# Scattering the experts' results to the tokens' places instead of gathering them, with weights fetched further ahead

## The chip, the cores and the metric

The kernel runs on one core of a Trainium2 chip. The core has a matrix engine (PE, with its weight loads shown apart as PEld), a vector engine (DVE), a scalar engine (ACT), GpSimd (POOL) and a queue engine (SP) that here only issues transfers. The engines run side by side and wait for each other through semaphores. The metric is the device time of one run in microseconds (us), the median over runs; lower is better.

## What is computed

Four layers, each a cross attention followed by a mixture of experts, both added to the stream `x` of 4 batches x 512 tokens x 128 channels. The context has 154 tokens per batch.

```python
x = x + L0_xattn(layernorm(x), ctx)                # one similarity, weights sim -> features -> W_qv
x = x + L0_ffn(layernorm(x))                       # 8 experts, the best 2 of each token, silu gate, hidden 512
x = x + L1_xattn(ctx, ctx, layernorm(x), mask)     # 16 heads of 8
x = x + L1_ffn(layernorm(x))                       # best 1 of 8, with a capacity, gelu, hidden 512
x = x + L2_xattn(layernorm(x), ctx)                # 16 heads of 64, gated
x = x + L2_ffn(layernorm(x))                       # best 2 of 8, gelu, hidden 256
x = x + L3_xattn(layernorm(x), ctx, ctx)           # 16 heads of 64
x = x + L3_ffn(layernorm(x))                       # best 2 of 8, relu, hidden 512

# an expert layer, in short
top_w, top_i = top_k(x @ Wg + bg, k);  w = softmax(top_w)
y[t] = sum over k of  w[t,k] * (act(x[t] @ W1[e] + b1[e]) @ W2[e] + b2[e])   with e = top_i[t,k]
```

## The kernel before

All arithmetic is in float32. A token tile is 128 tokens; there are 16 of them (`NT`), 4 per batch (`NI`). The stream `x` stays in SBUF.

**Experts by blocks.** Every expert layer is done in two halves, batches 0 and 1, then 2 and 3 (`NH` = 8 tiles each). `route` (L651) works out, for one half, which expert each token goes to and at which row of a DRAM buffer it is to lie, so that the rows of one expert fill whole blocks of 128. A half has a fixed number of blocks, `BLK`: 23 with two experts a token, 15 with one, which is enough for any routing; unused rows hold what was there before. `route` is a generator, advanced a step at a time beside other work. It ends with a list of `scatter` calls (L721): one GpSimd indirect transfer moves 128 normalized token rows to their rows of `buf`, 512 bytes each.

`experts` (L825) then walks over the blocks. `load` (L835) brings four blocks of token rows, after all scatters of the half; `tokens` transposes them; `up` (L855) reads the block's expert from a register on SP and PE, loads this expert's up weights into one of three `w` buffers and multiplies; `down` (L882) applies the activation, multiplies by the down weights and copies the result to `ys`, which SP stores as a block to `ybuf` (L928). `up` of a step is emitted ahead of `down` of the step before. A step is one block in layer 0 and two in the others (`PER`).

**Back to the tokens.** `gather` (L948) reads `ybuf` back by rows: for each of a half's tiles and each of its one or two experts, one GpSimd indirect transfer of 128 rows (L953), each after all stores of the half. `combine` (L965) adds the rows times the gate's weight to `x`.

**Order.** The main loop (L1356) emits: attention; the first half's experts, with the second half's routing beside them; the first half's gathers; the next layer's keys and values (`at.early`); the second half's experts, and between their steps the first half's combination, statistics (`stats`, whose last operation runs on POOL), normalization and queries (`at.late`); then the next layer's attention, beside whose first tiles the second half is gathered and combined. Indirect transfers are not started at once: they wait in `rows_due`, and `row_transfers` (L641) takes some off, each tied to a piece of other work. In attention (`narrow_period`, `wide_period`) PE, ACT and partly DVE run in the order written; elsewhere a scheduler orders what is emitted. Each engine, and each transfer queue, works in order. SP carries all plain transfers: weights, token blocks, result blocks, and in attention the reciprocal sums that go through DRAM (`rd`, `rep`, L346 and L348). POOL carries the indirect ones and `rstd` (L236).

## Time and profile before

| what | us |
|---|---|
| runs, median of 3 | 1359.35 (1351.47 to 1362.25) |
| the profiled execution | 1282.47 |
| its span, first to last instruction | 1280.8 |
| layer 0 attention | 0 to 106 |
| layer 0 experts, first and second half | 106 to 195, 195 to 262 |
| layer 1 attention, experts | 262 to 478, 478 to 575 |
| layer 2 attention, experts | 575 to 803, 803 to 911 |
| layer 3 attention, experts | 911 to 1125, 1125 to 1252 |
| after the last expert block | 1252 to 1281 |

The stage bounds are read off the timeline and are not sharp, since the stages overlap. The profile is one execution; the mean TensorE clock granted in it was 0.917 of full speed. The costliest indirect transfers in it are 112 scatters (L722, 109.6 us of POOL) and 112 gathers (L953, 106.7 us); SP issues 110 result stores (L928), 44 token loads (L840) and 168 loads of up weights (L869). A line of the profile reads: engine, line, operation, output and inputs, count; a bracket gives the idle time of the engine just before and what ended it.

### The profile page before, as it was taken

How to read it: one execution, taken by the hardware profiler on the slowest of the kernel's cores; microseconds unless marked ns; L12 is line 12 of the kernel's file. 1: busy time of each engine (PE TensorE's matmuls, PEld its weight loads, DVE VectorE, ACT ScalarE, POOL GpSimd, SP SyncE). 2: the span in 40 equal slices, each digit the busy share in tenths (PEclk: the TensorE clock that was granted, in tenths of full speed). 3: DMA queues.
4: the chain of work that ended last, by engine and by line, in shares of the span. 5: the costliest groups of instructions: out<-in, count | busy, mean ns of one | idle time of the engine just before them, and what ended most of it. 6: DMA issues, size and time to landing. Idle time of an engine off the chain costs nothing.

```text
span 1280.8 us, 26318 instructions
## 1 busy us (share of the span) xinstructions
PE 1089.4 (85%) x9351; PEld 896.9 (70%) x9351; DVE 731.6 (57%) x2012; ACT 565.3 (44%) x2264; POOL 253.6 (20%) x281
## 2 busy tenths in 40 slices
PE   4787998977878888889999998966899999899990
PEld 3657998933435448787878777855778788789890
DVE  6554646567666763335665776424476576646352
ACT  2113433454554543546656565321656665532230
POOL 2041315023000010232000004045220000402334
PEclk8767999988898988998999999887999999999996
DMA  7023786721100314433112214444421111334762
GB/s 228 1 81 113 216 253 189 207 94 25 23 19 26 100 38 119 133 110 84 35 35 55 64 37 123 123 150 133 127 55 45 41 35 35 109 95 143 209 191 60
DMA packets 136064, 126.77 MB, mean 99 GB/s; under 512 B 12538, under 2 KB 115583, under 8 KB 135551
## 3 DMA queue, kind: packets, MB, share of 16 engines
q1 hardware_dynamic: 128767, 110.39, 30.5%
q0 software_dynamic: 7168, 14.69, 3.9%
q8 instruction: 77, 1.26, 0.4%
q14 instruction: 52, 0.43, 0.1%
HBM read 101.31 MB, written 23.72 MB: 98 GB/s over the span
## 4 chain that ended last, share of the span: by engine, by line
PE 59%; DVE 12%; DMA 9%; issue 8%; ACT 5%; POOL 5%; SPq 2%; POOLq 0%; DVEq 0%
PE sc L877 11%; PE av L916 6%; PE tr L371 6%; PE sc L607 5%; PE av L408 5%; PE tr L425 5%; PE sc L592 3%; DMA yg<-ybuf,su 3%; POOL yg L953 3%; ACT probs L308 3%; DVE nm L294 3%; PE sc L1175 2%; DMA w<-in_up 2%; PE av L390 2%; PE tr L358 2%
## 5 line engine op out<-in xcount | busy, mean ns | idle before, releaser
L308 ACT ACTIVATE probs<-sc,nm 128x154 f32<-128x154 f32 x768 | 286.9, 403 | 162.7 <-DVE nm L294 162.5
L877 PE MATMUL sc<-tokT,w 128*128 128x128 f32 x1528 | 201.3, 286 | 8.7 <-DMA w<-in_up 3.6
L877 PEld LDWEIGHTS sc<-tokT,w 128*128 128x128 f32 x1528 | 189.0, 200 | 15.5 <-ACT eg L900 5.2
L294 DVE TENSOR_REDUCE nm<-sc 128x6 f32<-128x924 f32 x144 | 142.6, 1007 | 74.8 <-PE sc L607 49.1
L308 ACT ACTIVATION_READ_ACCUMULATOR probs<-sc,nm 128x1 f32 x768 | 168.3, 219 | 0.0
L916 PE MATMUL av<-w,hT 128*128 x1160 | 155.3, 279 | 3.2 <-DVE hT L905 2.5
L953 POOL DMA_INDIRECT yg<-ybuf,su x112 | 106.7, 952 | 246.5 <-ACT pT L267 59.9
L722 POOL DMA_INDIRECT buf<-xn,su x112 | 109.6, 979 | 227.0 <-DVE eb L745 97.3
L916 PEld LDWEIGHTS av<-w,hT 128*128 128x128 f32 x1160 | 141.9, 193 | 8.9 <-issue 4.7
L236 POOL TENSOR_TENSOR rstd<-ve,nhalf 128x4 f32<-128x4 f32 x32 | 33.0, 1032 | 547.3 <-DVE ve L234 429.6
L264 DVE COPY pT<-tr 128x512 f32<-128x512 f32 x160 | 106.9, 684 | 45.3 <-PE tr L371 41.5
L408 PE MATMUL av<-pT,vm 128*64 128x128 f32 (+1 forms) x1536 | 106.2, 284 | 22.5 <-DVE pT L264 22.4
L371 PE MATMUL tr<-ident,probs 128*128 128x128 f32 x768 | 123.1, 291 | 1.5 <-DVE rT L337 1.5
L371 PEld LDWEIGHTS tr<-ident,probs 128*128 128x128 f32 x768 | 86.1, 146 | 33.4 <-issue 21.7
L408 PEld LDWEIGHTS av<-pT,vm 128*64 128x64 f32 (+1 forms) x1536 | 63.8, 126 | 55.7 <-DVE pT L264 30.9
L900 ACT ACTIVATE eg<-sc,w 128x128 f32<-128x128 f32 x184 | 52.9, 368 | 89.5 <-PE sc L877 82.1
L607 PE MATMUL sc<-kT,qT 64*128 64x154 f32 x1024 | 87.1, 308 | 4.8 <-ACT probs L308 4.8
L905 DVE SCALAR_TENSOR_TENSOR hT<-sc,w,eg 128x128 f32<-128x128 f32 x184 | 56.2, 342 | 51.0 <-ACT eg L900 51.0
L607 PEld LDWEIGHTS sc<-kT,qT 64*128 64x128 f32 x1024 | 71.3, 189 | 15.8 <-issue 9.9
L592 PE MATMUL sc<-xnT,wq 128*128 128x128 f32 x512 | 73.6, 303 | 4.7 <-ACT probs L308 2.3
L592 PEld LDWEIGHTS sc<-xnT,wq 128*128 128x128 f32 x512 | 67.3, 212 | 10.2 <-issue 3.6
L425 PE MATMUL tr<-wo,aT 128*128 128x128 f32 x512 | 66.2, 284 | 1.6 <-DVE xnT L256 1.3
(255 smaller groups left out, 1432.2 us busy)
## 6 DMA issues: line engine op xcount, KB each, us to landing
w<-in_up SPq DMA_DIRECT2D x46, 516.0 KB
w<-in_up SPq DMA_DIRECT2D x76, 258.0 KB
rep<-rd SPq DMA_DIRECT2D x64, 256.0 KB
tok<-buf SPq DMA_DIRECT2D x36, 256.0 KB
ybuf<-ys SPq DMA_DIRECT2D x58, 128.0 KB
w<-in_down SPq DMA_DIRECT2D x3, 2048.0 KB
w<-in_up SPq DMA_DIRECT2D x46, 128.0 KB
ybuf<-ys SPq DMA_DIRECT2D x52, 64.0 KB
```

Of the source, the lines that this page charges most:

```text
L264: return nc.vector.tensor_copy(o, i)
L294: nc.vector.tensor_reduce(self.at.heads(self.nm, g, n), self.sc[g][:, :, 0 : n * S2].rearrange("p j (s k) -> p j s k", s=n), AX.X, ALU.max ...
L308: nc.scalar.activation(self.pr[:, h, :], self.sc[g][:, j, s * S2 : (s + 1) * S2], AF.Exp, bias=self.nm[:, h : h + 1], accum_out=self.rs[:, ...
L371: nc.tensor.transpose(q[:, t * P : (t + 1) * P], self.pr[:, h, 0:P], ident)
L408: nc.tensor.matmul(av[rows, cols], v, self.pT[n][:, t, :], start=False, stop=last)
L425: nc.tensor.matmul(o[:, 0:D], self.aT[:, c, :], self.at.wo[:, c, :], start=(c == 0), stop=(c == self.nb - 1))
L592: nc.tensor.matmul(sc[:, c // 4, c % 4 * P : (c % 4 + 1) * P], wq[:, c * P : (c + 1) * P], at.xnT[:, i * P : (i + 1) * P], start=True, sto ...
L607: nc.tensor.matmul(sc[:, j, s * S2 : (s + 1) * S2], at.qT[i][rows, c, :], at.kT[rows, c, :], start=True, stop=True)
L722: ins = nc.gpsimd.indirect_dma_start(out=buf[half], out_offset=bass.IndirectOffsetOnAxis(ap=su[:, t : t + 1], axis=0), in_=xns[t // NI][:, ...
L877: nc.tensor.matmul(dst, w[:, b, at : at + P], xT, start=True, stop=True)
L916: nc.tensor.matmul(y[:, b * D : (b + 1) * D], hT[:, fc, :], w2[:, bass.ds(es[b], 1), fc, :].rearrange("p o d -> p (o d)"), start=(fc == 0) ...
L953: ins = nc.gpsimd.indirect_dma_start(out=yg[:, t, :], out_offset=None, in_=ybuf[half], in_offset=bass.IndirectOffsetOnAxis(ap=su[:, t : t ...
```

## The change

Results take the other way. A token row in `buf` gets two more columns: the token's place in the output and the row of its first expert. When a block is loaded, two DVE operations make of these the row of `ybuf` where each result belongs (`goal`): two rows for a token, one per expert. Rows of no token, or left over from an earlier layer, come out beyond the end. Each block's result then goes to `ybuf` by one indirect transfer on POOL, with a bounds check that skips those rows. The half comes back in plain loads on SP, one a batch, after all results of the half. The gathers and the plain stores are gone.

With it:

- the halves of layer 0 become batch 0, and batches 1 to 3 (15 and 31 blocks); the routing of the second half is taken batch by batch and begun earlier; layer 0's attention gets a written PE order;
- up weights are fetched in groups of one or two steps, alternately into `w` and into a buffer of attention's `probs`, three groups ahead, instead of one step at a time;
- results wait in `results_due`, at most six steps; while scatters are due, these go first, two plus the step's blocks at a time;
- the next layer's first scores are made before the last experts are finished, and the first tokens of a second half wait for the next layer's values on PE;
- several small buffers become single or shared.

```diff
+GROUPS = (((0,), (1, 2, 3)), ((0, 1), (2, 3)), ((0, 1), (2, 3)), ((0, 1), (2, 3)))
+ROW = D + 2
+ROWS = 2 * B * S
+LAG = 6
...
     def route(layer, half, wg, bg, b2):
...
+        for some in ([b] for b in batches) if layer == 0 or half else (batches,):
...
+                rows = rt.tile([P, NI, ROW], F32, tag="xn", name="rows", bufs=4)
+                new.append(norm(x[b], f, rows))
+                nc.vector.tensor_scalar(
+                    rows[:, :, D], place[:, b * NI : (b + 1) * NI], float(-(layer + 1) * ROWS), None, ALU.add
+                )
...
+            if k == 0:
+                for n, rows in enumerate(xns):
+                    nc.vector.tensor_copy(rows[:, :, D + 1], sl[:, n * NI : (n + 1) * NI])
...
-    def experts(layer, half, routed, w2):
+    def experts(layer, half, routed, w2, ahead=()):
...
+        few = UP_WIDTH // (per * width)
+        groups, at = [], 0
+        while at < len(turns):
+            big = len(groups) > 1 and len(groups) % 2 == 0
+            groups.append((turns[at : at + few * (1 + big)], big))
+            at += len(groups[-1][0])
...
+        def fetch(k):
...
+            if big:
+                w = p2.tile([P, H, S2], F32, tag="probs", name="w_more").rearrange("p h k -> p (h k)")
+            else:
+                w = wff.tile([P, UP_WIDTH], F32, tag="w", name="w")
...
+                    nc.sync.dma_start(v[:, b, :], pack[bass.ds(e, 1), :, :].rearrange("o p n -> p (o n)"))
...
+            second = small.tile([P, 4], F32, tag="second", name="second")
+            nc.vector.tensor_tensor(
+                second[:, 0:m], tok[:, 0:m, D + 1], slot[:, 4 * g : 4 * g + m], ALU.not_equal
+            )
+            goal = small.tile([P, 4], U32, tag="goal", name="goal", bufs=6)
+            nc.vector.scalar_tensor_tensor(
+                goal[:, 0:m], tok[:, 0:m, D], float((layer + 1) * ROWS), second[:, 0:m], ALU.add, ALU.add
+            )
...
-            ys = p3.tile([P, 2, D], F32, tag="ys", name="ys")
-            row_transfers(
-                2 * n, nc.vector.tensor_copy(ys[:, 0:n], y[:, 0 : n * D].rearrange("p (b d) -> p b d", b=n))
+            ys = p3.tile([P, 2, D], F32, tag="ys", name="ys", bufs=LAG + 2)
+            done = nc.vector.tensor_copy(ys[:, 0:n], y[:, 0 : n * D].rearrange("p (b d) -> p b d", b=n))
+            results_due.extend(partial(result, j, ys[:, b, :]) for b, j in enumerate(blocks))
+
+            some = min(len(rows_due), 2 + n)
+            row_transfers(some, done)
+            results(2 + n - some)
+            results(len(results_due) - LAG * n)
+
+        def result(j, y):
+
+            ins = nc.gpsimd.indirect_dma_start(
+                out=ybuf[half],
+                out_offset=bass.IndirectOffsetOnAxis(ap=goals[j // 4][:, j % 4 : j % 4 + 1], axis=0),
+                in_=y,
+                in_offset=None,
+                bounds_check=ROWS - 1,
+                oob_is_err=False,
             )
-            rows = ybuf[half][blocks[0] * P : (blocks[0] + n) * P, :]
-            stores.append(nc.sync.dma_start(rows.rearrange("(b p) d -> p b d", p=P), ys[:, 0:n]))
...
-    def gather(half, routed, stores):
...
-    def combine(half, k, i, routed, got):
...
+    def combining(layer, half, routed, stores):
...
+        def get(k):
+            b = batches[k]
+            yg = p2.tile([P, NI, top, D], F32, tag="yg", name="yg")
+            rows = ybuf[half][2 * b * S : 2 * (b + 1) * S, :].rearrange("(i p c) d -> p i c d", p=P, c=2)
+            wait_for(nc.sync.dma_start(yg, rows[:, :, 0:top, :]), stores, "any block may hold these tokens")
+            return yg
+
+        got = {k: get(k) for k in range(min(2, len(batches)))}
...
+        first, second = (Steps(route(layer, half, *gates[layer])) for half in range(2))
+        with tc.manual_schedule(engines={mybir.EngineType.PE}):
+            tiles = [prepare(b, found[b]) for b in range(2)]
+            tiles[0].step()
+            tiles[0].finish()
...
+        second = Steps(experts(layer, 1, routed[1], w2, early)).step((3, 2, 2, 2)[layer])
+
+        while len(stores) < most_blocks(layer, 0) and second.taken < 8:
+            second.step()
+        results(most_blocks(layer, 0) - len(stores))
+        combined = Steps(combining(layer, 0, routed[0], stores)).step()
+        for k, b in enumerate(GROUPS[layer][0]):
+            combined.step(NI // 2)
...
+            second.step(-(-most_blocks(layer, 1) // PER[layer]) - second.taken)
+            at.tile = Tile(at, 0)
+            at.tile.score(0)
+            at.tile.most(0)
         stores = second.finish()
-        beside = Steps(combining(1, routed[1], gather(1, routed[1], stores)))
+        results()
+        beside = Steps(combining(layer, 1, routed[1], stores)).step()
```

## The prediction

> **What bounds the kernel now.** I read the page's busy shares first, then busy time by stage, then the waits, then the chain inside the two worst stages. The page says who is loaded:
>
> ```profile
> PE 1089.4 (85%) x9351; PEld 896.9 (70%) x9351; DVE 731.6 (57%) x2012; ACT 565.3 (44%) x2264; POOL 253.6 (20%) x281
> ```
>
> TensorE leaves 1280.8 - 1089.4 = 191 us idle; nothing else is near full. The change touches no attention or expert product, so it can only work on those 191 us. Where they lie, by stage (columns: stretch, length, then busy time of PE, PEld, DVE, ACT, POOL with counts, granted clock, DMA share, GB/s):
>
> ```profile
> 0.00:106.00 106.00, 69.16 (x318) 53.69 (x318) 61.49 (x252) 16.67 (x55) 29.25 (x49) 0.74 0.32 98
> 106.00:195.00 89.00, 86.71 (x732) 84.36 (x733) 46.28 (x178) 36.60 (x114) 16.43 (x17) 0.96 0.71 213
> 262.00:322.00 60.00, 42.10 (x291) 19.89 (x294) 40.39 (x99) 31.30 (x155) 17.43 (x18) 0.89 0.20 61
> 322.00:478.00 156.00, 129.14 (x1013) 68.38 (x1013) 105.62 (x228) 77.07 (x374) 10.98 (x11) 0.89 0.16 42
> 846.00:890.00 44.00, 21.82 (x147) 18.81 (x147) 15.16 (x49) 6.71 (x12) 23.15 (x25) 0.78 0.52 148
> 1252.00:1281.00 29.00, 0.00 (x0) 0.00 (x0) 5.70 (x16) 0.00 (x0) 15.13 (x16) 0.57 0.21 59
> ```
>
> Layer 0's experts (106 to 195) already keep PE 97% busy. The holes are layer 0's attention with its first token wait, the first 60 us of layer 1's attention (42.1 busy; at the 129.14/156 of the rest it would do the same in 51), the change of halves in layer 2 (22 of 44 us empty) and the tail, 29 us without PE. Their waits (engine and line, what it waited for: us, times, longest):
>
> ```profile
> DVE x L971 <- DMA yg<-ybuf,su: 59.5, 58, 6.4
> PE tr L850 <- DMA tok<-buf: 22.4, 6, 10.1
> PE sc L877 <- DMA w<-in_up: 3.6, 6, 1.2
> ```
>
> So gathers and scatters stand behind the holes; the up weights stop PE for 3.6 us only. The indirect transfers, from the timeline of layer 2 and of the tail:
>
> ```profile
> 852.81 0.96 POOL L722 DMA_INDIRECT buf<-xn,su  x1 [0.30 <-issue]
> 854.07 0.96 POOL L722 DMA_INDIRECT buf<-xn,su  x1 [0.30 <-issue]
> 859.38 1.97 PE L850 MATMUL tr<-ident,tok 128*128 128x128 f32 x8 [10.14 <-DMA tok<-buf]
> 889.22 0.48 PE L251 MATMUL tr<-ident,xn 128*128 128x128 f32 x1 [10.17 <-DVE xn L243]
> 1251.11 0.29 DVE L925 COPY ys<-av 128x128 f32<-128x128 f32 x1 [0.33 <-PE av L916]
> 1255.38 0.95 POOL L953 DMA_INDIRECT yg<-ybuf,su  x1 [22.54 <-issue]
> 1274.13 0.94 POOL L953 DMA_INDIRECT yg<-ybuf,su  x1 [0.30 <-issue]
> ```
>
> One indirect transfer takes POOL 0.96 + 0.30 = 1.26 us, so sixteen gathers are 20 us in a row, and they start only when a half's last block is stored. That row of twenty is what the change attacks.
>
> **What goes and what comes.** The 112 gathers and the 110 plain stores of results go. Come: 168 indirect writes of one block (46 + 30 + 46 + 46 by layer), 56 POOL instructions more, and plain loads, one a batch (16, of 512 or 256 KB). An indirect write moves the same 64 KB as a scatter, so I price it at the scatter's 1.26 us, landing 2.3 to 3.3 us after its start (the chain has 2.25 at 101.17 and 3.33 at 529.55). A bounds check is in no row. From below it costs nothing, or gains a little since a third of the rows is skipped (21,504 slots for 14,336 results). From above I allow another 0.95, a second pass over the indices: 2.2 us. I take 1.26.
>
> Here a rule speaks against the change. 112 gathers are 939/947/1047 ns (shortest, median, longest), also between 920 and 940 us where DVE is busy 13.6 of 20. The Trainium skill ("SBUF — State Buffer", its warning on DVE blocking DMA under SBUF: two separate sides, and A bandwidth-pool intuition that's wrong) says that GpSimd-issued DMAs starve while DVE holds the shared port, 620 ns alone becoming about 3100. By the rule a write would be up to 1.26 + 2.5 = 3.7 us and the change would lose well over 100 us; by the row it does not occur with this kernel's DVE work. I use the row.
>
> A loaded batch of 512 KB costs about 4.6 us (a 516 KB weight load is 4.49 to 4.86 in the chain around 160 to 212).
>
> Token rows grow from 512 to 520 bytes. Loads of four blocks land in about 2.7 us (103.57 to 106.3). The skill ("DMA: Bandwidth & Descriptors", How a descriptor splits into AXI transactions) says reads that start off a 256-byte boundary fetch extra; its 576-byte example goes from 18 to 25 beats, so I estimate up to 40% on the moving part, some 0.5 us, exposed at the eight starts of a half: 4 us. By the trace's aligned rows it is nothing. I leave it in the range.
>
> **Stage by stage**, on the profiled execution:
>
> 1. Layer 0's first tokens: 6.46 us before L850 at 106. With one batch in the first half, its eight scatters go out under the other batches' attention. -5. The new hand-written PE order of this attention could do anything from -10 to +8; PE is at clock 0.74 there and idle 37 us in all. I take -2.
> 2. Layer 0's change of halves gets worse. A block is 1.79 + 0.89 + 0.27 = 2.95 us of PE (up, down, transpose), so the new first half is 15 x 2.95 = 44 us. The second half's 24 scatters are only emitted from about the seventh block on (20 us), three a block, with two results among them: 26 x 1.26 = 33 us, then 2.3 landing and 2.7 load: 58 us. PE waits 58 - 44 = 14, of which the next layer's values fill 3 to 4. Today there is no such gap. +10.
> 3. Weights ahead: L877's waits and the late starts behind them between 160 and 220 (PE 54.3 of 60 busy). The SP queue no longer holds L928, which waited there for L905 and L925 124 us in all, ahead of the next weights. PE was mostly covered. -3.
> 4. Start of layer 1's attention: 60 us of work that fits in 51. The DVE queue there stands behind L971, with PE's pT, softmax and residual copies behind it. Two loads landing together take that away; 8 combines more move in (8 x 0.35 = 2.8). -5.
> 5. Layer 1's experts (478 to 575) leave 10.6 us of PE idle. Tokens 1.8, tokT 1.6, norms 1.1 to 1.8; eight gathers (10 us) become one load. Routing has batch 2 done early. -6.
> 6. Layers 2 and 3 start with scores already made: gaps of 2.79 at 578 and 1.96 + 1.43 at 909 to 911. -5.
> 7. Layer 2's experts: first gap. The scatters (834.9 to 855) start perhaps 3 us earlier, as four of eight norms are done before: 10.1 becomes 7. Second gap: POOL must now issue 16 scatters and 15 results after 831, 31 x 1.26 = 39 us, to 870; landing 872, load 877, eight combines, statistics and norm 885, against 888.8 now. More expert steps are placed ahead of it (ten of 2.33 us from 857: 880). 10.2 becomes about 5. PE runs less cold (0.57 in 880 to 900): -2. Together -10.
> 8. Layer 3's change of halves (2.39 at 1201): -2.
> 9. Tail: results of the last three blocks 1250.5 to 1254.2, landed 1256.5, first batch 1261, second 1263.5, eight combines each, last at 1267 against 1277. -10.
>
> Sum: -5 -2 +10 -3 -5 -6 -5 -10 -2 -10 = -38. Added DVE work (two small operations per four blocks, 43 x about 0.4 us, and row tags) is hidden by DVE's idle half in the expert stages; if DVE filled up, 17 us would be its worst.
>
> **A new wait.** Each plain load waits on the SP queue for a half's last result. Behind it stand weights, tokens and, at a layer's start, `rep` and `rd` for the first tile. Three groups of weights are fetched ahead, so 4 us of waiting is covered in the second halves. After layer 2, POOL (23 x 1.26 = 29 us from 870) ends about 899 and SP is free at 902; PE enters attention at about 893 and needs `rep` about a tile (13 us) later. Just covered.
>
> **Rivals.** (a) POOL becomes the bound. In layer 2 a block is 1.16 us of PE and a result 1.26 of POOL, so nothing absorbs a higher price. At 2.2 us: after 831 POOL needs 20 + 38 x 2.2 = 104 us, to 935, and SP's loads hold back attention's `rep` by about 20 us beside 10 more for batch 0; in layer 3, 46 x 2.2 + 20 = 121 us against 98 of PE, 20 at the tail; layers 0 and 1 about 3. That is 53 us: -38 + 53 = +15, or 1375. It turns from gain to loss at 1.26 + 0.94 x 38/53 = 1.9 us a write. For it: no row prices the check, POOL is in order and statistics' rstd stands in the same queue. Against it: rows of indirect transfers do not vary.
> (b) The waits are hidden anyway or return as the gap in step 2 doubled and a worse PE order in layer 0's attention: -38 + 12 + 8, and half of steps 4 to 6 lost (8): -10, about 1349. For it: PE is 85% busy and gathers were partly beside other work.
> (c) The transfer does not skip rows, so it does what it did with a third more bytes: 64 KB each as now. That alone costs about nothing.
>
> **Numbers.** The profiled execution took 1282.47 us (span 1280.8), the runs 1359.35 in the median, 6% more; the trace does not say why. 38 us off are 1321 if carried over as they are and 1359.35 x 1244.5/1282.5 = 1319 in proportion. I say 1320. Its own range, with step 2 between 0 and +20, layer 0's order and the 520-byte rows: 1292 to 1345. Chances: forecast 0.67, (a) 0.17, (b) and (c) 0.16. Runs of this kernel differ by 0.8%, so about 1% is what can be told from no change: below 1346 faster, above 1373 slower. Of (a), 0.14 lie above 1373 and 0.03 below; of (b) and (c), 0.01 below 1346, 0.02 above 1373: faster 0.68, same 0.16, slower 0.16. The range, 1283 to 1368, leaves out some 0.05 below and 0.15 above.
>
> **What would show it.** Right: L953's twenty-microsecond rows gone; indirect writes to ybuf near 0.96 us; the tail after the last PE instruction near 20 us instead of 29.7; the 10 us gaps at layer 2's halves at 7 and 5; a new PE gap near 10 us at layer 0's change of halves. Wrong: an indirect write above 1.9 us, SP waiting tens of us for results at a layer's start, or layer 0's attention longer than 106 us.

## The result, and the profile after

| kernel | us, median (range) | to before |
|---|---|---|
| before | 1360.38 (1351.47 to 1362.25) | |
| after | 1394.45 (1390.44 to 1400.99) | 1.0268, 95% interval 1.0208 to 1.0329 |

The change costs 34 us. The profiled execution of after had a span of 1391.3 us. The page of after, busy shares, chain and the two groups of indirect transfers:

```profile
PE 1116.0 (80%) x9351; PEld 916.3 (66%) x9351; DVE 735.9 (53%) x2132; ACT 564.0 (41%) x2264; POOL 311.7 (22%) x339
...
PE 61%; DVE 14%; issue 7%; DMA 5%; another core or an unknown queue 4%; ACT 4%; SPq 3%; POOL 1%; POOLq 0%; DVEq 0%; ACTq 0%
...
L1031 POOL DMA_INDIRECT ybuf<-ys,goal x168 | 165.3, 984 | 271.0 <-DVE ys L1021 140.7
...
L778 POOL DMA_INDIRECT buf<-rows,su x112 | 108.8, 971 | 221.9 <-DVE pT L287 112.8
```

POOL's price is as forecast: 984 ns for an indexed write with a bounds check, beside 971 for a scatter. New is an entry of the chain, "another core or an unknown queue", 4% of the span (56 us); the page of before that the prediction read had none (a second profile of before, e1 below, has 4% too). Busy time by stage, after (columns as before: stretch, length, PE, PEld, DVE, ACT, POOL, granted clock, DMA share, GB/s):

```profile
140.00:160.00 20.00, 17.74 (x137) 16.86 (x136) 8.47 (x31) 4.93 (x17) 10.48 (x11) 0.91 0.39 126
160.00:180.00 20.00, 5.15 (x27) 3.96 (x25) 1.42 (x5) 1.14 (x4) 13.85 (x16) 0.62 0.29 97
180.00:200.00 20.00, 9.98 (x48) 9.24 (x49) 6.63 (x24) 2.87 (x9) 3.69 (x4) 0.52 0.55 171
200.00:220.00 20.00, 19.97 (x171) 19.18 (x171) 14.21 (x57) 7.80 (x26) 6.96 (x7) 1.00 0.47 150
...
900.00:920.00 20.00, 2.32 (x11) 1.58 (x10) 0.69 (x1) 0.48 (x1) 14.36 (x15) 0.64 0.32 94
```

At both changes of halves (layer 0 at 160 to 200, layer 2 at 900 to 920) PE, DVE and ACT mostly stand and POOL works; DMA is busy 0.29 to 0.55 of the time. After 200, with a result written every 2.9 us, PE is full. A wait for tokens would look the same in this view. The timeline of layer 2's stretch, after, tells the two apart:

```profile
896.59 16.39 SPq L917 DMA_DIRECT2D w<-in_up  x8
898.87 0.96 POOL L778 DMA_INDIRECT buf<-rows,su  x1 [0.30 <-issue]
...
903.78 0.40 PE L972 MATMUL sc<-tokT,w 128*128 128x128 f32 x2 [1.14 <-issue]
905.91 0.37 PE L972 MATMUL sc<-tokT,w 128*128 128x128 f32 x1 [1.73 <-issue]
...
921.47 0.42 DVE L1021 COPY ys<-av 128x256 f32<-128x256 f32 x1 [14.84 <-remote]
923.72 0.60 ACT L983 ACTIVATE hT<-sc 128x512 f32<-128x512 f32 x1 [21.52 <-remote]
924.37 2.08 PE L1013 MATMUL av<-w,hT 128*128 x8 [16.66 <-issue]
```

Sixteen scatters occupy POOL from 898.9 to 918.8. PE is still among the first half's products then (L972, L1013), whose tokens it has; yet it passes one in one or two microseconds without a named reason and then none for 16.66, ACT and DVE wait for "remote" (a release that the trace cannot name), SP needs 16.39 us for eight loads of weights that took it 7.26 in another trace of the same kernel (e7 below), and PE, DVE and ACT resume 3 to 6 us after the last scatter. The tail did get shorter: PE ends at 1375.1, 16.2 us before the span does (29.7 in before).

The runs below were made on six chips, with before run beside them on each: before takes about 1276 us on chips 11 and 14 and about 1350 on chips 0, 10, 13 and 15, so each ratio is taken on one chip, and "at 1276" and "at 1350" say which kind it is. The profile of before that the prediction read is of the first kind, the measurement of the result of the second. No wait for "remote" stands in any of the nine traces at 1276; each of the eleven at 1350 has some. No run moves a kernel from one kind to the other: the chip, or something that went with it, may be what differs.

Not all of the difference is standing. PE's own busy time is 1116.0 us in after and 1080.2 in e7, the same kernel at 1276, so 36 of the 93 us between the two spans lie in the same products taking longer; the mean granted clock is 0.887 against 0.918. Within after it is 1.00 at 200 to 220, where PE is full, and 0.52 to 0.64 in the stretches where PE mostly stands. Stage by stage (PE's first transposition of tokens in a layer bounds a stage; us, one profiled execution each, at 1276 or at 1350; e1, e7 and e18 are runs told of below):

| stage | before, at 1276 | after, at 1276 (e7) | before, at 1350 (e1) | after, at 1350 | results stored plainly, at 1350 (e18) |
|---|---|---|---|---|---|
| start to layer 1's first tokens | 479.6 | 496.8 | 485.5 | 513.5 | 501.3 |
| to layer 2's | 323.8 | 330.0 | 341.2 | 347.9 | 343.4 |
| to layer 3's | 337.9 | 340.6 | 372.2 | 381.5 | 354.9 |
| to the end | 139.5 | 131.1 | 151.0 | 148.4 | 141.8 |
| span | 1280.8 | 1298.5 | 1349.8 | 1391.3 | 1341.3 |

### The profile page after: what moved, and what is told of

It reads as the page before. It is cut to its first block, busy times and chain, and to the rows that moved or that the text cites. A ratio compares the mean times of both kernels' runs of the same rounds, so it can differ in the third digit from the quotient of the medians.

```text
span 1391.3 us, 26439 instructions
## 1 busy us (share of the span) xinstructions
PE 1116.0 (80%) x9351; PEld 916.3 (66%) x9351; DVE 735.9 (53%) x2132; ACT 564.0 (41%) x2264; POOL 311.7 (22%) x339
## 4 chain that ended last, share of the span: by engine, by line
PE 61%; DVE 14%; issue 7%; DMA 5%; another core or an unknown queue 4%; ACT 4%; SPq 3%; POOL 1%; POOLq 0%; DVEq 0%; ACTq 0%
PE sc L972 12%; PE av L1013 9%; PE tr L396 6%; PE av L433 6%; PE sc L635 5%; PE tr L450 4%; PE sc L1297 2%; PE sc L620 2%; DVE nm L317 2%; PE av L415 2%; ACT probs L331 2%; PE tr L383 2%; PE tr L944 1%; DVE x L1087 1%
## 5 line engine op out<-in xcount | busy, mean ns | idle before, releaser
L1031 POOL DMA_INDIRECT ybuf<-ys,goal x168 | 165.3, 984 | 271.0 <-DVE ys L1021 140.7
L1013 PE MATMUL av<-w,hT 128*128 x1160 | 163.6, 288 | 43.3 <-issue 18.2
L1013 PEld LDWEIGHTS av<-w,hT 128*128 128x128 f32 x1160 | 148.4, 200 | 52.6 <-issue 23.6
L778 POOL DMA_INDIRECT buf<-rows,su x112 | 108.8, 971 | 221.9 <-DVE pT L287 112.8
L972 PE MATMUL sc<-tokT,w_more 128*128 128x128 f32 x888 | 121.1, 287 | 9.6 <-issue 8.6
L972 PEld LDWEIGHTS sc<-tokT,w_more 128*128 128x128 f32 x888 | 113.0, 203 | 12.3 <-issue 10.4
L972 PE MATMUL sc<-tokT,w 128*128 128x128 f32 x640 | 90.0, 295 | 14.4 <-issue 8.0
L1021 DVE COPY ys<-av 128x256 f32<-128x256 f32 (+1 forms) x110 | 38.8, 355 | 111.9 <-PE av L1013 61.0
L972 PEld LDWEIGHTS sc<-tokT,w 128*128 128x128 f32 x640 | 83.7, 208 | 17.8 <-issue 9.3
L620 PE MATMUL sc<-xnT,wq 128*128 128x128 f32 x512 | 69.9, 293 | 4.9 <-ACT probs L331 4.0
```

Source lines behind the costliest of these rows:

```text
L620: nc.tensor.matmul(sc[:, c // 4, c % 4 * P : (c % 4 + 1) * P], wq[:, c * P : (c + 1) * P], at.xnT[:, i * P : (i + 1) * P], start=True, sto ...
L778: ins = nc.gpsimd.indirect_dma_start(out=buf[half], out_offset=bass.IndirectOffsetOnAxis(ap=su[:, t : t + 1], axis=0), in_=xns[t // NI][:, ...
L972: nc.tensor.matmul(dst, w[:, b, at : at + P], xT, start=True, stop=True)
L1013: nc.tensor.matmul(y[:, b * D : (b + 1) * D], hT[:, fc, :], w2[:, bass.ds(es[b], 1), fc, :].rearrange("p o d -> p (o d)"), start=(fc == 0) ...
L1031: ins = nc.gpsimd.indirect_dma_start(out=ybuf[half], out_offset=bass.IndirectOffsetOnAxis(ap=goals[j // 4][:, j % 4 : j % 4 + 1], axis=0), ...
```

## The experiments

### Before once more, and with longer rows (e1, e2)

e1 is the kernel before without an edit. e2:

```diff
-    buf = [dram.tile([BLK[0] * P, D], F32, name=f"buf{h}") for h in range(2)]
+    buf = [dram.tile([BLK[0] * P, ROW], F32, name=f"buf{h}") for h in range(2)]
...
-    zero = const.tile([P, D], F32, name="zero")
+    zero = const.tile([P, ROW], F32, name="zero")
```

with ROW = D + 2, token tiles as wide, and the two columns set to zero.

> The kernel before, unchanged, profiled once more, since its one profiled execution took 1282 us and its timed runs about 1360. If the profiled execution was one of a faster kind, this one takes about 1360 and shows where 78 us more lie. Theory A (long streams of indirect writes hold up the other engines, whatever the row length): the gaps of the profile after near the scatters of a second half (PE stepping one matmul at a time, 17 us at layer 2) show here too. Theory B (the 520-byte rows do it): the scatters here disturb no other engine, as in the first profile.

> The kernel before with only the rows of buf lengthened from 512 to 520 bytes (two zero columns; token loads and scatters carry them). Theory B (520-byte rows, off the 512-byte grid, slow the scatters' writes and hold up the other engines): slower by 1 to 3%, 15 to 40 us, with PE gaps of 5 to 20 us while the sixteen scatters of a half run. Theory A (the order and number of POOL's transfers): within 0.5%.

e1 took 1351.49 us; its PE timeline in layer 2, and the windows of the same sixteen scatters in the first profile and then in e1:

```profile
873.81 2.08 PE L916 MATMUL av<-w,hT 128*128 x8 [8.61 <-issue]
...
881.74 2.08 PE L916 MATMUL av<-w,hT 128*128 x8 [5.00 <-DVE ys L925]
```

```profile
835.00:855.00 20.00, 13.83 (x100) 11.29 (x98) 4.34 (x9) 4.69 (x9) 15.26 (x16) 0.96 0.54 164
```

```profile
858.00:878.00 20.00, 10.13 (x70) 8.66 (x68) 1.54 (x3) 2.26 (x5) 15.19 (x16) 0.79 0.37 116
```

So the stop beside a row of scatters (POOL 858 to 878 there) is in the unchanged kernel too. The execution of 1282 us that the prediction was built on did not have it: nearly all that PE lacks in its window belongs to the wait for tokens (10.14 us, to 859.38) that the prediction shows. It is not the row's length: e2 is 0.98% above before (ratio 1.0098, 1.0071 to 1.0124), 13 us, and their largest piece is of another kind. SP's timeline of e2, then of e1:

```profile
15.48 8.73 SPq L825 DMA_DIRECT2D w<-in_down  x1
```

```profile
15.14 5.29 SPq L822 DMA_DIRECT2D w<-in_down  x1
```

The zero fill of the token buffers, one 520-byte piece a row, stands in front of the down weights. Behind them come the small loads of layer 1; PE then stands 11.89 us at 41.67 (1.54 in e1), and layer 0's first tokens come 11.2 us later (118.26 against 107.09). At layer 1's first tokens 5.7 us of this are left (491.2 against 485.5); the spans differ by 11.1 again (1360.9 against 1349.8) because 5.5 us more are lost after layer 3's first tokens, where both traces have stops beside rows of transfers. So the fill is seen, but not that it makes up all of the 13 us.

### Rows of transfers that nobody needs (e6, e14, e15)

To separate the transfers from all that waits for them, before gets 96 indirect writes of zeros into memory that nothing reads, under the attention of layers 2 and 3: in e6 and e14 (the same kernel) as six rows of 16, in e15 one at a time.

```diff
+    def stream():
+        at = small.tile([P, 1], U32, tag="sink_at", name="sink_at")
+        nc.vector.tensor_copy(at, lane)
+        for sink in sinks:
+            nc.gpsimd.indirect_dma_start(
+                out=sink, out_offset=bass.IndirectOffsetOnAxis(ap=at[:, 0:1], axis=0), in_=zero, in_offset=None
+            )
...
                     def after(b=b, i=i, step=step):
                         step()
+                        if layer > 1 and (b, i) in ((1, 1), (1, 3), (2, 2)):
+                            stream()
```

> The kernel before, with six rows of 16 indirect writes each added on POOL, to places of memory that nobody reads, in the middle of the attention of layers 2 and 3, where POOL has nothing else to do and nobody waits for it. Each row takes POOL 16 x 1.26 = 20 us. Theory A (a row of indirect transfers holds the other engines up) expects PE to have idle time put down to issue or to remote while such a row runs, 3 to 20 us each, and the time 20 to 100 us above before. Rival E (an indirect transfer costs only POOL and those that wait for it) expects less than 6 us above before, and PE as busy in these stretches as in the ones beside them.

> The kernel before with six rows of 16 unread indirect writes under the attention of layers 2 and 3, once more. Where before takes about 1276 us it has measured 0.6% above before. Where before takes about 1350 us, theory A (there a row of indirect transfers stops the other engines until it ends) expects idle PE of 8 to 20 us beside each of the six rows and 40 to 110 us (3 to 8%) above before; rival E (a row costs POOL alone there too) again less than 1%.

> The same 96 unread indirect writes, but each released by one of the copies of the attention (four in a tile of some 15 us), so that POOL pauses between them. Theory A with rows as the cause expects less than 1.5% above before wherever it runs; if each indirect transfer stops the other engines by itself, rows or not, it costs as much as the six rows do.

| run | before on the same chip | ratio (interval) | added, of the medians |
|---|---|---|---|
| e6, six rows | 1275.75 | 1.0059 (1.0037 to 1.0082) | 9.6 us |
| e14, six rows | 1349.64 | 1.0876 (1.0827 to 1.0925) | 121 us |
| e15, one at a time | 1349.64 | 1.0470 (1.0412 to 1.0527) | 64 us |

The stretch of one row of 16 in layer 3, in e6 and then in e14 (windows):

```profile
1021.00:1041.00 20.00, 20.00 (x220) 17.56 (x219) 11.61 (x17) 13.11 (x56) 15.43 (x16) 1.00 0.40 103
```

```profile
1140.00:1160.00 20.00, 8.90 (x87) 6.96 (x87) 3.97 (x6) 5.73 (x26) 14.68 (x16) 0.74 0.26 73
```

The same code and the same 16 transfers: PE full in one execution, at 8.9 of 20 us in the other, with DVE and ACT down as well. The waits of e14 name it only as:

```profile
DVE pT L264 <- remote: 93.1, 14, 11.5
```

Six rows hold POOL 96 x 1.27 = 122 us, and the time grows by 121 (118 by the ratio): here a row of indirect transfers costs about its whole length, although nobody waits for its data. At 1276 it costs 1.6 us a row. Spacing does not cure it: 64 / 96 = 0.67 us each in e15, where less than 1.5% in all was expected if rows were the cause. So rows are not needed for it; they are only the worse case. (e15 was not run at 1276.) The transfers themselves are no slower for it: the DMA engines are less busy in e14's stretch, 0.26 to 0.40, and by the two pages the indirect packets take 4.8% of 1467.2 us in e14, 70 us, and 5.8% of 1287.7, 75 us, in e6. It is not a fixed fee of a transfer either: the results of layer 0's second half in after, one every 2.9 us (200 to 220 above), left PE at 19.97 of 20.

### The indexed writes alone (e5, e18, e9)

In e5 and e18 (the same kernel) after's 168 results are stored by SP, one block after another, and everything else of the change stays.

```diff
-            ins = nc.gpsimd.indirect_dma_start(
-                out=ybuf[half],
-                out_offset=bass.IndirectOffsetOnAxis(ap=goals[j // 4][:, j % 4 : j % 4 + 1], axis=0),
-                in_=y,
...
+            base, n = 2 * S * GROUPS[layer][half][0], 2 * NI * len(GROUPS[layer][half])
+            for k in (j, j + 1) if j + 1 == nj < n else (j,):
+                at = base + k % n * P
+                ins = nc.sync.dma_start(ybuf[half][at : at + P, :], y)
```

> The kernel after, with the 168 results stored by plain transfers on SP's queue, block after block, in place of the indexed writes on POOL. It leaves out that results go to their tokens' places, so the sums are taken over wrong rows. Theory A (rows of indirect transfers on POOL stall the other engines) expects POOL's rows half as long, the stalls at the changes of halves of layers 0 and 2 cut to half or less, and 20 to 45 us less than after: 1350 to 1375. Rival C (the results' transfers are harmless, the second halves are held by the scatters and by the start-up alone) expects within 8 us of after. Rival D (SP's queue was what the indexed write relieved) expects SP to wait for results ahead of weights and tokens and the time to be above after by 5 us or more.

> The kernel after with its 168 results stored by plain transfers on SP's queue, in place of the indexed writes, as in the earlier run of it (it leaves out that results go to their tokens' places). Where before takes about 1276 us it measured 1.1% above before, 0.7% below after. Where before takes about 1350 us, each indirect transfer has stopped the other engines for 0.66 us (spaced) to 1.2 us (in rows); if that is what the indexed writes add there, taking 168 away brings 40 us or more: at least 2.5% below after, level with before or faster. If the indexed writes are not what costs there, it stays within 1.5% of after, so above 1.2% over before.

At 1276, e5 is 1.0105 (1.0073 to 1.0137), against 1.0171 for after. At 1350, e18 is 1.0021 (0.9999 to 1.0044), against 1.0268: 0.0247 x 1352 = 33 us, give or take 9 by the two intervals, or 0.2 us a write (the two ratios are of different chips). That is about the size of the measured loss, but not because the rest of the change costs nothing: e18 also has none of before's 112 gathers, which are indirect transfers too, and against e1 it loses 16 us before layer 1's first tokens and wins 26 after layer 2's first tokens (table above). At 1276 the writes' share is 8 us (0.0066 x 1277, give or take 7). 27 of the 50 us between the traces of after and e18 lie in layer 2's experts and the attention after them. e18's chain keeps 2% for the unknown queue; 112 scatters remain in it. The writes carry no more than a scatter does, and it is not a slower POOL: in e6 and e14 an added write takes 968 ns alike (median).

e9 goes the other way: everything of the change except the writes, with before's gathers in their place.

```diff
+PLACED = ()
...
+            if (layer, half) in PLACED:
+                results_due.extend(...)
+            else:
+                rows = ybuf[half][blocks[0] * P : (blocks[0] + n) * P, :].rearrange("(b p) d -> p b d", p=P)
+                stores.append(nc.sync.dma_start(rows, ys[:, 0:n]))
...
+                        ins = nc.gpsimd.indirect_dma_start(
+                            out=yg[:, i, c, :],
```

> The kernel after with everything of it but the indexed writes of results: blocks are stored by plain transfers to their own places and gathered by tokens as in before; halves, routing in steps, weights ahead, 520-byte rows and orders stay as after. If the indexed writes are what loses (56 more POOL transfers, in a row with the scatters), this is 10 us or more faster than after. If they gain at the tail and lose nothing elsewhere, it is 5 to 15 us slower than after. If the loss lies in the parts around them (start-up, uneven halves), it is within 5 us of after.

1.0294 (1.0245 to 1.0343) at 1276, 17 us above after: 16 of them in layer 3 (147.0 us from its first tokens to the end, 131.1 in e7). So at 1276 indexed writes are the better way for this layer's results. The gathers are not paced as in before, so e9 overstates it.

### After at 1276, and its start-up (e7, e4)

e7 is after without an edit; e4 writes the zeros in pieces of seven rows:

```diff
-    zero = p2.tile([P, ROW], F32, tag="rows", name="zero")
+    zero = w1.tile([P, 8, D], F32, tag="wo", name="zero").rearrange("p c d -> p (c d)")[:, 0 : 7 * ROW]
...
-        nc.sync.dma_start(buf[half].rearrange("(p c) d -> p c d", p=P), bc(zero, 1, MOST_BLOCKS[half]))
+        flat = buf[half].rearrange("(p c) d -> p (c d)", p=P)
+        for c in range(0, MOST_BLOCKS[half], 7):
+            n = min(7, MOST_BLOCKS[half] - c) * ROW
+            nc.sync.dma_start(flat[:, c * ROW : c * ROW + n], zero[:, 0:n])
```

> The kernel after, unchanged, to have its time and its trace beside the runs of this call. Theory A' (the loss has fixed places: about 12 us of start-up behind the short pieces of the zero fill, 14 to 18 us at layer 0's change of halves, 6 to 10 us at layer 2's, against about 10 us won at the tail) expects 2 to 3.5% above before also where before takes about 1276 us, with PE's gaps in those three places. Rival F (the loss needs the stalls of all engines that the traces of the longer runs show) expects, where before takes about 1276 us, less than 1% above before.

> The kernel after, with the zero fill of the token buffers written from a wider tile of zeros: seven rows in a piece, 3640 bytes, in place of one row of 520 bytes. If the start-up gap of PE (14.30 us ending at 48) comes from the short pieces that hold up the SP queue and the small loads behind them, the issue of layer 0's down weights falls from 13.4 us to under 6, the gap falls to under 4 us, and the time falls by 10 to 14 us, to about 1381 to 1385. If it comes from the new order of work in layer 0's attention, the gap and the time stay (within 4 us).

e7: 1301.02 us, 1.0171 (1.0128 to 1.0214). So 22 us of loss need no stopped engines. PE's gaps in e7 (timeline; the bracket is the idle time):

```profile
45.34 0.80 PE L1199 MATMUL av<-wc,xnT 128*128 128x128 f32 x2 [12.70 <-DVE wc L1191]
...
178.47 1.86 PE L944 MATMUL tr<-ident,tok 128*128 128x128 f32 x7 [19.09 <-DMA tok<-buf]
...
290.45 1.12 PE L396 MATMUL tr<-ident,probs 128*128 128x128 f32 x4 [8.31 <-DVE rT L362]
...
888.17 2.06 PE L944 MATMUL tr<-ident,tok 128*128 128x128 f32 x8 [13.05 <-DMA tok<-buf]
...
910.78 0.48 PE L274 MATMUL tr<-ident,xn 128*128 128x128 f32 x1 [10.35 <-DVE xn L266]
```

e4: 1302.59, 1.0200 (1.0157 to 1.0243), no gain where 10 to 14 us were expected. The first gap is gone, but in its PE timeline stands:

```profile
101.33 1.11 PE L944 MATMUL tr<-ident,tok 128*128 128x128 f32 x4 [8.30 <-DMA tok<-buf]
...
173.21 1.97 PE L944 MATMUL tr<-ident,tok 128*128 128x128 f32 x8 [17.80 <-DMA tok<-buf]
```

PE arrives earlier and waits for tokens instead; 3 us are left at layer 1's first tokens, and none at the end. Two things are in this. The tile of zeros became free only late, so the fill ran from 79.5 to 88 us: it was out of the way of the small loads, but the first scatters waited 6.1 us for it. And the lead over e7, 2.3 us at the first tokens and 5.3 at the second half's, melts by layer 2's first tokens, where e4 is 1 us behind; the traces do not show why. So e4 confirms what opens the first gap; what a fill that is neither in the way nor late would bring was not measured.

### Layer 0's halves and the order on POOL (e3, e8, e10, e11, e17, e12, e16)

e3, e8, e11 and e17 (the last two the same kernel) make layer 0's halves even:

```diff
-GROUPS = (((0,), (1, 2, 3)), ((0, 1), (2, 3)), ((0, 1), (2, 3)), ((0, 1), (2, 3)))
+GROUPS = (((0, 1), (2, 3)), ((0, 1), (2, 3)), ((0, 1), (2, 3)), ((0, 1), (2, 3)))
```

e3 leaves the written PE order alone and so routes batches 2 and 3 on `x` from before their attention. e8 routes each behind its attention and has e4's (late) fill; e11 drops these steps, so that the second half is routed beside the first half's experts.

> The kernel after, with layer 0's halves even again (batches 0 and 1, then 2 and 3). Theory A (the stalls of the other engines go with long rows of indirect transfers on POOL; at layer 0's change of halves 24 scatters and 15 results stand in a row against 15 blocks of experts) expects the stall of 20 to 30 us between 160 and 195 gone or moved beside more blocks: 15 to 28 us less than after, about 1368 to 1380 us. Rival B (the stall there is that of the start-up or of the new order of layer 0's attention) expects within 6 us of after, and may be slower because the first tokens are waited for again (some 5 us). In the trace A expects PE busy 18 or more of each 20 us in layer 0's experts.

> The kernel after with both: layer 0's halves even, each batch's routing behind its attention, and the zero fill in pieces of seven rows. Theory A' expects both gaps gone, the start-up's 14 us and the 18 us at layer 0's change of halves, and a wait for the first tokens of about 5 us back: 18 to 28 us less than after, so 0 to 1.2% above before. If the gap only moves to another place of layer 0, it stays at more than 1.5% above before.

> The kernel after with layer 0's halves even and its second half routed only beside the first half's experts, as in before, so that no norm of the attention stands behind scatters on POOL. If the uneven halves are what opens the 19 us gap (15 blocks of 2.95 us are too few to cover the second half's scatters), the gap goes, a wait of about 5 us for the first tokens comes back, and the time is 8 to 16 us below after: 0.5 to 1.1% above before. If 19 us of waiting turns up at another place of layer 0 again, the time stays within 4 us of after (1.7% above before, or 2.7% where before takes about 1355 us).

> The kernel after with layer 0's halves even and routed as in before, beside before in this call. Where before takes about 1276 us: no gap at the change of halves, some 5 us for the first tokens, and 0.5 to 1.1% above before; if the gap turns up elsewhere in layer 0, 1.5% or more. Where before takes about 1350 us: as measured, about 2.4% above before.

At 1276: e3 1.0220 (1.0175 to 1.0265), e8 1.0245 (1.0188 to 1.0301); neither is better than after. In e8 the gap moved (PE timeline, then POOL's):

```profile
127.51 1.16 PE L274 MATMUL tr<-ident,rows 128*128 128x128 f32 x4 [19.53 <-DVE rows L266]
```

```profile
125.94 1.04 POOL L258 TENSOR_TENSOR rstd<-ve,nhalf 128x4 f32<-128x4 f32 x1
```

A norm for the router ends with an operation on POOL, and that one stood behind the first half's 16 scatters: 20 us, of the size of the gap that was removed. e11 and e17 take that norm out of the attention, but both ran at 1350: 1.0240 (1.0177 to 1.0302) and 1.0165 (1.0118 to 1.0212), against after's 1.0268. There is no gap at the change of halves any more, 3 to 4 us for the first tokens, and layer 1's first tokens come at 499.5 and 492.8 instead of 513.5. So the uneven halves cost 14 to 21 us of a trace at 1350, though by the ratios only the second run stands off from after, and barely. What e11 brings at 1276 was not measured.

e10 had the halves and fill of e8, and gathers everywhere except in layer 3's second half.

> Even halves in layer 0 and the wide zero fill, results stored plainly and gathered in all halves but the last one of layer 3, which alone keeps the indexed writes and plain loads. It keeps the only place where the change gained, the tail: expected 8 to 12 us below before there if the rest is as before, so 0.5 to 1% faster than before; if the other parts of the change (520-byte rows, routing in steps, weights ahead) cost by themselves, it is level with before or slower.

1.0318 (1.0266 to 1.0370) at 1276: with e8's new gap in it (21.8 us) and e9's unpaced gathers it tells nothing of the tail.

e12 and e16 (the same kernel) keep the uneven halves and hand over the second half's scatters in one row; the results, which then wait, get room for nine steps (`LAG = 9`), and two blocks of layer 0 share a buffer:

```diff
-            some = min(len(rows_due), 2 + n)
-            row_transfers(some, done)
-            results(2 + n - some)
-            results(len(results_due) - LAG * n)
+            row_transfers()
+            results(2 + n if n == 2 else 3)
```

> The kernel after with the uneven halves kept, but the second half's scatters handed to POOL in one row as soon as their places are known, with no results between them (results of two blocks of layer 0 share a buffer, so that they can wait). At layer 0's change of halves 8 results x 1.29 = 10 us leave the row in front of the tokens: if POOL's order is what sizes the gap, it falls from 19 us to 5 to 9 us, at layer 2's from 13 to about 10, and the time by 10 to 16 us, to 0.5 to 1% above before. If the scatters' start or the loads behind them size it, it stays above 15 us and the time within 4 us of after.

> The kernel after with the second half's scatters in one row, as in the earlier run of it, beside before in this call. Where before takes about 1276 us: the gap at layer 0's change of halves falls from 19 us to 5 to 9 and the time to 0.5 to 1% above before, if POOL's order sizes the gap. Where before takes about 1350 us: as measured, about 2.9% above before.

Both ran at 1350: 1.0294 (1.0235 to 1.0354) and 1.0337 (1.0280 to 1.0394), no gain. Windows of e12:

```profile
120.00:140.00 20.00, 19.86 (x177) 18.65 (x175) 14.74 (x67) 9.53 (x25) 8.11 (x10) 1.00 0.58 192
140.00:160.00 20.00, 7.18 (x31) 5.58 (x31) 1.38 (x2) 1.62 (x5) 15.12 (x17) 0.61 0.16 53
160.00:180.00 20.00, 12.05 (x91) 12.00 (x92) 7.28 (x29) 3.42 (x12) 8.69 (x9) 0.71 0.39 124
```

The scatters are done at 164.7 instead of 180.8. But the row of 24 stops the first half's blocks while it runs, and the second half's first tokens come at 191.9, where after has 192.9. PE's last wait before them is 7.42 us in e12 and 5.27 in after: at 1350 the stopped blocks hide what POOL's order does to the gap of 19.09 that e7 has. Whether this order pays at 1276 is open.

### The tail alone (e13)

Before, with indexed results, tagged rows and plain loads only in layer 3's second half:

```diff
+            if tail:
+                for b, j in enumerate(blocks):
+                    ins = nc.gpsimd.indirect_dma_start(
+                        out=ybuf[half][0:ROWS, :],
+                        out_offset=bass.IndirectOffsetOnAxis(ap=goals[j // 4][:, j % 4 : j % 4 + 1], axis=0),
...
+                        bounds_check=ROWS - 1,
```

> The kernel before with the indexed results, the plain loads and the tagged 520-byte rows only in the second half of layer 3, where nothing follows (a token buffer of its own, zeroed in large pieces under layer 1). The tail's sixteen gathers go: if the gain at the tail is real and stands alone, the time after the last PE instruction falls from about 29 to about 14 us and the time by 8 to 15 us, so 0.6 to 1.1% below before. If it is given back (results between layer 3's scatters and gathers on POOL, or the tags), the time is within 4 us of before.

At 1350: 1.0066 (1.0037 to 1.0096), so a little slower. After the last PE instruction stand 19.4 us instead of 29.4 (e1), so the 10 us are won, but in the half before it PE loses more. One window of e13, from the middle of that half:

```profile
1281.00:1301.00 20.00, 12.88 (x74) 11.28 (x73) 5.53 (x19) 4.02 (x13) 13.38 (x14) 0.74 0.37 108
```

Fourteen transfers in 20 us, and PE at 12.9. From layer 3's first tokens to the end e13 takes 156.0 us, e1 151.0. None of the versions beats before where it was run.

## Why the prediction was wrong

**Two steps failed.** Between the forecast, 38 us won, and the result, 34 lost, lie 72 us.

The first is the price of an indirect write: "I price it at the scatter's 1.26 us", a cost of POOL alone, that lies beside PE unless tokens wait for it. POOL's part was right (0.98 and 0.30). What such a transfer takes from the other engines, where the result was measured, was put at nothing: it is up to 1.26 us in rows, 0.67 spaced in attention, 0.2 net on average over the 168 writes, together about 33 us (e18). A warning was in the numbers: the profiled execution stood 6% under the runs, and "the trace does not say why" was followed by carrying the sum over as if the 6% touched no part of it. Before has 224 indirect transfers of its own, and its two profiled spans differ by 69 us, half of it (34) from layer 2's first tokens to layer 3's, where e1 shows the stops.

The second is the sum itself. With the writes taken out, e18 still loses 3 us where 38 were to be won, 41 of the 72. And at 1276, where no stop shows, after loses 22, so 60 us are missing there. The largest part is the sum of steps 1 to 4, -5: up to layer 1's first tokens after is 17 us later than before at 1276 (e7), and e18 is 16 later than e1 at 1350.

**Rival (a)** had the right engine and the wrong reason. It made POOL the bound above 1.9 us a write; a write took 1.28. The Trainium skill's rule weighed there ("SBUF — State Buffer", two separate sides, and A bandwidth-pool intuition that's wrong: DVE's hold on the shared port starves GpSimd's transfers) was rightly not used: a write takes POOL 984 ns on average in after, and the longest single indirect transfer of all traces is 2.39 us (e12), below the page's 3100 ns. What the runs at 1350 show points the other way: DVE, ACT and PE stand, and SP is late, while POOL issues at its usual pace.

**The steps at 1276**, against e7, where the loss of 22 is 18 between the profiled spans, by stages:

- *Steps 1 to 4, start to layer 1's first tokens: -5 predicted, +17 measured.* Step 2 named the right place with too small terms. The second half's scatters were to start 20 us into the half and to have 2 results among them; they started at 134.1, 30.5 us after the first tokens (103.65), with 6 results among them, and so landed and loaded 74.8 us after those, not 58. The gap is 19.09, not 14. Of step 1's 7 us, order included, 2.7 came (103.65 against 106.34), beside a new start-up gap of 12.70 and a norm waiting 6.5 us at 97. That the 520-byte rows matter in the fill was not seen: "DMA: Bandwidth & Descriptors" (How a descriptor splits into AXI transactions) was applied to loads alone, 4 us; e2 has 13, and the piece of it that the traces show lies in the fill. Step 4's 5 us did not come: PE is busy 41.2 of the 60 us from 272 (42.1 in before, from 262), with one wait of 8.31 at 290, where DVE's queue still stands behind the combination (L1087), which waits 3.39 us for the loaded batch.
- *Steps 5 and 6, layer 1's experts and layer 2's attention: -11 predicted, +6 measured.* No run separates it. The norm of layer 1's second half waits 4.3 us on PE at 522, where before had 1.5.
- *Step 7, layer 2: -10 predicted, +3 measured.* The scatters did not start 3 us earlier but 5.5 later in the stage (863.8 - 826.8 = 37.0 against 31.5): POOL stands from 850.8 to 858.7 and then issues four results first. Gaps 13.05 and 10.35, not 7 and 5.
- *Steps 8 and 9, layer 3: -12 predicted, -8 measured.* The tail was right: L953's row gone, 15.7 us after PE's end in e7.

Rival (b), waits that return, describes this part, but at +22 and not -10. Step 3, weights ahead, was not tried by itself. The tail's term came as forecast; the new gap at layer 0's change of halves came in its place, but larger.

## What to carry to other kernels

Price a transfer not only by the engine that issues it: put a row of idle ones under work that doesn't need it, and read whether the other engines slow down. When the one profiled execution is several per cent off the runs, the difference belongs to some mechanism, and a change that multiplies what sets it can be worth more than all that the profile shows; profile again first. And a shift of one queue's order has to be followed to every short operation behind it, such as a norm's last step on POOL behind 20 us of scatters.

## What was not expected of the hardware

- At 1350, 96 indirect writes that nothing waits for added 121 us in rows and 64 us spaced; at 1276 the same rows added 9.6. A write in a row takes POOL 968 ns in both (medians). Why the two kinds differ, and what holds the engines, is not shown by any run.
- While a row runs at 1350, PE passes single products within a group whose inputs are long there, and the trace names no wait of the program for them. Many of their starts lie 1.4, 2.1, 2.8 or 3.5 us apart (after, e12, e16), multiples of about 0.70.
- Two columns more in a token row, 520 bytes for 512, cost 13 us (e2): with the zero fill in such pieces, the issue of the load behind it took 8.73 us for 5.29, and the first tokens came 11 us later, of which 6 were left a layer on.
